# Gate product in four parts, square in two, and a rescheduled first layer, in a two-layer image kernel

## The chip, the cores and the metric

The kernel runs on one core of a Trainium2 chip. The metric is the device time of one execution in microseconds (us), the median of several runs. The engines are named as in the profile: PE (TensorE, matrix products; its weight loads are listed apart as PEld), DVE (VectorE), ACT (ScalarE), POOL (GpSimd) and SP (SyncE, which issues nearly all transfers). Each engine works through its own queue in order.

## The reference

The input is a batch of 4 images with 128 channels and 64 x 64 pixels. Layer 0 is a convolutional block with state-space branches, layer 1 is attention with a mixture of experts. All of it is in float32. The change lies in layer 0, whose core is the gated scan that the reference calls `_mamba`:

```python
def _mamba(x, in_w, in_b, conv_w, conv_b, A_log, D, dt_bias, rms_w, out_w, headdim, d_state):
    zxbcdt = x @ in_w.T + in_b
    z = zxbcdt[..., :di]
    xBC = zxbcdt[..., di:2 * di + 2 * d_state]
    dt = jax.nn.softplus(zxbcdt[..., -nh:] + dt_bias)
    xBC = sum((xp[:, k:k + l, :] * conv_w[:, k] for k in range(K)))
    xBC = _silu(xBC + conv_b)
    ...
    y = _ssd(xs * dt[..., None], dt * A, Bm, Cm)
    y = y + D[None, None, :, None] * xs
    y = y.reshape(b, l, di) * _silu(z)
    y = y * jax.lax.rsqrt(jnp.mean(y * y, -1, keepdims=True) + 1e-05) * rms_w
    return y @ out_w.T

def _ssd(x, A, Bm, Cm, chunk=64):
    Lmat = jnp.exp(_segsum(A))
    Yd = jnp.einsum('bcln,bcsn,bhcls,bcshp->bclhp', Cm, Bm, Lmat, x)
    dec = jnp.exp(Acs[..., -1:] - Acs)
    states = jnp.einsum('bcln,bhcl,bclhp->bchpn', Bm, dec, x)
    ...
    Yo = jnp.einsum('bcln,bchpn,bhcl->bclhp', Cm, prev, jnp.exp(Acs))
    return (Yd + Yo).reshape(b, l, h, p)
```

The line `y.reshape(b, l, di) * _silu(z)` is the gate product of the title, and `y * y` in the line below it is the square. Around the branches, layer 0 has a group norm, a projection to 8 seed channels, layer norms and, per image, a convolution block: a product that widens 128 channels to 256, a 3 x 3 depthwise convolution, a gelu and a product back to 128.

## The kernel before

**Tiling.** A sequence of 4096 pixels is worked on in 8 blocks of 512 positions (`LB`), and a block in chunks of 64 (`Q`). One item is one block of one scan. There are 72 items: 8 of the seed scan (all four images together, 4 lanes) and 64 of the cascade (two scans in a row for each of 4 images and 8 blocks, 8 lanes). For a cascade item the main tiles hold 128 partitions x 1024 elements, for a seed item 128 x 512: four parts `u` (`NU` = 4) of 256 or 128 elements.

**Stages of an item** (class `Mamba`). `outer` loads and normalizes the block. `prep` loads it again with its halo (tile `x4`, four transfers on SP's queue from the scratch tensor `hl`) and makes the decays: `ps_dt`, `u`, `sd`, the scan `acs`, and `cdx`, `ps_cd`, `cds`. `front` computes z, x, B and C on PE (`ps_z`, `ps_x`, `ps_B`, `ps_C`), each closed by a silu on ACT; then the transposes `pt_b` and `pt_x`, the products `ps_g` with their mask (tile `gm`), the states `ps_st`, the two scans `cd` over them on DVE (with the small product `inj` and an addition into `ps_st` between the first and the second), and `ps_yo`, the part of y that comes from earlier states. The state at the end of an item is kept in `last` for the next item of the same scan. `back` does the part inside the chunks and the closing.

**The closing of `back`.** For each part `u`, `exponentials(u)` makes the decay factors e (PE `ps_d`, then an exponential on ACT), `weigh(u)` multiplies them by `gm` on DVE, and `within(u)` multiplies them with x on PE and adds the result to y on DVE, in four instructions. In the profile the psum tiles of `within` are named `bank` and in the code `py`. After all four parts, one POOL instruction multiplies the gate into the whole tile (`zs` <- `y`, `zs`), one ACT instruction squares it (`y` <- `zs`), PE takes the mean (`ps_ms`, four instructions), ACT makes the reciprocal root out of it, and PE the product `ps_out`.

**The order of the work** in layer 0 is neither written out by hand nor left to the compiler. The class `Deck` records every instruction with the tiles that it reads and writes; `flush` then plays a model of the five engines and emits the instructions in the order in which the model starts them. Each operation has a price (`price`; `SIDE` holds PE's prices for some psum tiles). When an operation ends, those that need it become ready after `LAG` us on another engine; what a transfer brings is ready `LAND` us after it. Among the ready operations of an engine the one of the highest rank goes first. The rank is the place in the record, moved back by `BEHIND`, a table by stage, engine and tile: 120 means "as if recorded 120 places later", -200 means earlier. `NEAR` lets PE look, among operations of nearly the same rank, for one of the same shape of weights; it is 0. `lockers` keeps POOL's instructions and DVE's with two inputs in SBUF from running at the same time in the model. The rest follows from the rings of buffers: a tile can be opened only when one of its ring is free.

**Layer 0's end and layer 1.** The convolution block (function `ffn`) of one image runs beside the scans of the next. For the last image there is no next: its block runs alone with the first projections of layer 1 (`early`), recorded and flushed separately. In it `merge(k)` loads and normalizes block k into a tile of the ring `outs`, `expand` and the taps compute on it, and `close` finishes the block and frees the tile. `depth` adds buffers to the rings `outs` and `acc`; `load` fetches input blocks into the ring `xg`. Layer 1 is written in a fixed order and isn't touched.

Of the kernel before, what the change touches and what calls it, by code (L numbers as in the profile page):

```python
# [20 lines left out]
F32 = mybir.dt.float32  # L21
# [10 lines left out]
LB = 512  # L32
# [243 lines left out]
class Mamba:  # L276
# [344 lines left out]
    def back(self, it, out):  # L621
# [59 lines left out]
        for u in range(NU):  # L681
            within(u)
            if u + 1 < NU:
                weigh(u + 1)
            if u + 2 < NU:
                exponentials(u + 2)
            yield


        nc.gpsimd.tensor_mul(zs, y, zs)  # L690
        yield
        yield
        nc.scalar.activation(y, zs, AF.Square)
        yield
# [69 lines left out]

SIDE = {"py": 0.0435, "ps_yo": 0.033, "ps_d": 0.08}


class Deck:
# [67 lines left out]
    def price(self, engine, name, args, kw, out, ins, op):  # L836
# [26 lines left out]
        if engine == "gpsimd":  # L863
            return 0.15 + 0.0023 * n
        quick = name in ("tensor_scalar", "tensor_copy") and len(sb) == 1 and out.space == bass.MemoryType.SB
# [6 lines left out]
    BEHIND = {  # L872
        ("back", "gpsimd", "last0_casc1"): 120, ("back", "scalar"): -50, ("back", "scalar", "A_casc1"): -200,
        ("back", "scalar", "e"): -40, ("back", "sync", "gfd"): -10, ("back", "sync", "hl"): 120,
        ("back", "sync", "raw"): -40, ("back", "sync", "td"): 110, ("back", "tensor", "ps_d"): -70,
        ("back", "tensor", "py"): 120, ("back", "vector", "A_casc1"): -200, ("back", "vector", "bdt_casc1"): 70,
        ("back", "vector", "biasB_casc1"): 40, ("back", "vector", "wc_casc1"): -120, ("ffn", "scalar"): 10,
        ("ffn", "tensor", "ps_mean"): 40, ("ffn", "vector", "acc"): 140, ("front", "gpsimd"): 220,
        ("front", "gpsimd", "last_casc1"): -10, ("front", "scalar"): 20, ("front", "scalar", "Bc"): 50,
        ("front", "scalar", "Cc"): -200, ("front", "scalar", "cd"): 200, ("front", "scalar", "zs"): -70,  # L880
        ("front", "tensor"): 20, ("front", "tensor", "ps_ea"): -120, ("front", "tensor", "ps_g"): -120,
        ("front", "tensor", "ps_st"): -20, ("front", "tensor", "pt_x"): 40, ("front", "vector", "gm"): 10,
        ("front", "vector", "ps_st"): -20, ("front", "vector", "xd"): -200, ("front", "vector", "xp0"): -10,
        ("outer", "gpsimd"): -200, ("outer", "gpsimd", "halo_seed"): 200, ("outer", "gpsimd", "last0_casc0"): 120,
        ("outer", "scalar"): 40, ("outer", "scalar", "hi"): -120, ("outer", "scalar", "ln_r"): -20,
        ("outer", "sync", "raw"): 20, ("outer", "sync", "wc_seed"): 20, ("outer", "sync", "xin"): -40,
        ("outer", "tensor"): 110, ("outer", "tensor", "ps_tok"): 40, ("outer", "vector"): -20,
        ("outer", "vector", "A_seed"): 200, ("outer", "vector", "W_casc0"): 200, ("outer", "vector", "bdt_casc0"): 10,
        ("outer", "vector", "bdt_seed"): 10, ("outer", "vector", "biasB_casc0"): 20,
        ("outer", "vector", "biasB_seed"): -10, ("outer", "vector", "biasx_seed"): 200,  # L890
        ("outer", "vector", "raw"): 70, ("prep", "gpsimd"): 70, ("prep", "gpsimd", "cdx"): 10,
        ("prep", "gpsimd", "halo_seed"): 10, ("prep", "gpsimd", "x4"): -40, ("prep", "scalar", "cde"): -70,
        ("prep", "sync", "x4"): 40, ("prep", "tensor", "ps_cd"): 10, ("prep", "vector", "acs"): -190,
        ("prep", "vector", "sdT"): -70,
    }
    LAG = 0.2
    NEAR = 0
    LAND = 4.0

    def flush(self, tc):  # L900
# [29 lines left out]
        for i, op in enumerate(ops):  # L930
            if op.waits == 0:
                heappush(events, (0.0, 0, i))
        now, table, lock, mode = 0.0, None, None, None
        lockers = {"vector": 0.0, "gpsimd": 0.0}
        while events:
# [16 lines left out]
            for e in engines:  # L952
# [3 lines left out]
                while ready[e]:  # L956
# [12 lines left out]
                    if any(room[r] < k for r, k in need.items()) or any(  # L969
# [6 lines left out]
                        continue  # L976
                    if e == "tensor" and chosen is None and op.mode != mode:

                        chosen = key
                        continue  # L980
                    if chosen is not None and (op.mode != mode or key[0] - chosen[0] > self.NEAR):
                        aside.append(key)
                        if key[0] - chosen[0] > self.NEAR:
                            break
                        continue
                    if chosen is not None:
                        aside.append(chosen)
                    chosen = key
# [16 lines left out]
                if e == "tensor" and op.mode != mode:  # L1005
                    mode = op.mode
                    start += 0.1
                if e == "scalar":
                    if op.set == SILU:
                        phases[op.phase] -= 1  # L1010
                        lock = op.phase if phases[op.phase] else None
                    if op.set is not None and op.set != table:
                        table = op.set
                        start += 1.3
                end = start + op.cost
                busy[e] = end
# [128 lines left out]
def layer0(tc, T, td, const, ident, eps, where, batches, qkv):  # L1145
# [9 lines left out]
    with ExitStack() as ctx:  # L1155
# [62 lines left out]

        def load(b, k, work=work):
            xin = work.tile([128, LB], F32, tag="xg", bufs=4, name="xin")  # L1220
            nc.sync.dma_start(out=xin, in_=T["x"][b, :, blk(k)])
            return xin
# [125 lines left out]
        def ffn(b, work, ps, depth=0, diag=0, taps=None, ps_taps=None):  # L1348
# [18 lines left out]
            def merge(k):  # L1367
# [13 lines left out]
                nc.sync.dma_start(out=gf, in_=gfd[32 * b:32 * b + 8, blk(k)])  # L1381
                xg = load(b, k, work)
                yield
# [49 lines left out]
            def conv(k):  # L1433

                accs[k] = []
                for g in range(2):
                    acc = work.tile([128, LB], F32, tag="acc", bufs=3 + depth, name="acc")
                    sums = made[k].pop(0) if k in made else None
                    for i in range(diag, 9):
                        w = P("dw")[:, 9 * g + i:9 * g + i + 1]  # L1440
                        if sums is None:
                            nc.vector.tensor_scalar(rows(acc), tap(g, i), w, None, ALU.mult)
                        else:
                            nc.vector.scalar_tensor_tensor(rows(acc), tap(g, i), w, sums, ALU.mult, ALU.add)
                        sums = rows(acc)
                        if i % 3 == 2:
                            yield
                    accs[k].append(acc)

            def close(k):  # L1450
# [4 lines left out]
                nc.scalar.preload_act_table_set(LNEXP)  # L1455
                xin = load(b, k, work)
                yield
# [73 lines left out]

        pending = deck.staged("ffn", ffn(pending, last, single("f", 4), 0, 4, taps, single("t", 2)))
        run((pending, FFN), (deck.staged("early", early()), 5 * NBLK + 7))
# [503 lines left out]
```

## Time and profile before

Three runs took 8400.1, 8414.19 and 8424.57 us: a median of 8414.19 us.

| | before |
|---|---|
| median of three runs | 8414.19 us |
| the profiled execution | 8410.01 us |
| its span, first to last instruction | 8408.0 us |
| granted TensorE clock over the span | 0.948 |
| busy over the span: PE / DVE / ACT / POOL | 7635.6 / 6326.8 / 5095.5 / 4737.9 us |
| gate product `zs` on POOL, 64 cascade items | 160.8 us, 2513 ns each |
| square `y` <- `zs` on ACT, 63 of the cascade items | 66.6 us, 1057 ns each |
| `ps_ms` on PE, 252 instructions of cascade items | 118.7 us busy |
| `ps_out` on PE, as many, the same shapes | 79.6 us busy |

The first five rows are of the whole execution; the others are of the stretch from 150 to 3550 us, which holds nearly all of the items. The profile records one execution. Its times are microseconds, "mean ns" is the mean of one instruction. Every recorded instruction of layer 0 carries line 1031, since the scheduler emits them all there; so groups are told apart by the names of their tiles. "Idle before, and what ended it" gives the time that an engine stood still ahead of the instructions of a group, and the instruction on another engine that released it. The granted clock is the share of its full rate at which PE was allowed to run.

### The profile page before, as it was taken

How to read it: one execution, taken by the hardware profiler on the slowest of the kernel's cores; microseconds unless marked ns; L12 is line 12 of the kernel's file. 1: busy time of each engine (PE TensorE's matmuls, PEld its weight loads, DVE VectorE, ACT ScalarE, POOL GpSimd, SP SyncE). 2: the span in 40 equal slices, each digit the busy share in tenths (PEclk: the TensorE clock that was granted, in tenths of full speed). 3: DMA queues.
4: the chain of work that ended last, by engine and by line, in shares of the span. 5: the costliest groups of instructions: out<-in, count | busy, mean ns of one | idle time of the engine just before them, and what ended most of it. 6: DMA issues, size and time to landing. Idle time of an engine off the chain costs nothing.

```text
span 8408.0 us, 191225 instructions
## 1 busy us (share of the span) xinstructions
PE 7635.6 (91%) x80284; PEld 4548.2 (54%) x80284; DVE 6326.8 (75%) x11211; ACT 5095.5 (61%) x6444; POOL 4737.9 (56%) x3225
## 2 busy tenths in 40 slices
PE   5888888888888888789999999999999999999998
PEld 3566666666666666534554555555555545555554
DVE  6767667887788788767777777777777777777775
ACT  5767677777777777654555555555555555555554
POOL 1111111111111111107999999999999999999997
PEclk8899899988999999889999999999999999999999
DMA  4211111121121112135454545454545545444442
GB/s 143 84 51 45 54 47 50 54 56 50 51 58 52 51 54 57 34 122 132 125 133 125 130 118 138 120 127 128 127 122 132 131 120 131 118 119 119 120 120 60
DMA packets 306604, 800.54 MB, mean 95 GB/s; under 512 B 43984, under 2 KB 61008, under 8 KB 288848
## 3 DMA queue, kind: packets, MB, share of 16 engines
q1 hardware_dynamic: 304848, 780.94, 35.3%
q8 instruction: 633, 10.37, 0.5%
q10 hardware_dynamic: 432, 5.12, 0.2%
q0 software_dynamic: 464, 2.25, 0.1%
q14 instruction: 227, 1.86, 0.1%
HBM read 595.19 MB, written 192.94 MB: 94 GB/s over the span
## 4 chain that ended last, share of the span: by engine, by line
PE 51%; POOL 25%; DVE 10%; ACT 7%; issue 5%; DMA 2%; SPq 0%; POOLq 0%; DVEq 0%; ACTq 0%
POOL s L1885 14%; PE ps_mx L1841 7%; POOL es L1887 6%; PE acc L1900 6%; PE ps_s L1879 5%; PE bank L1031 4%; PE ps_s L1873 3%; PE ps_x L1031 2%; PE ps_B L1031 2%; PE ps_d L1031 2%; DVE y L1031 2%; PE ps_C L1031 2%; PE ps_yo L1031 2%; DVE e L1031 2%; POOL zs L1031 1%
## 5 line engine op out<-in xcount | busy, mean ns | idle before, releaser
L1843 DVE TENSOR_REDUCE mx<-ps_mx 128x1 f32<-128x512 f32 x4096 | 2789.4, 688 | 818.8 <-PE ps_mx L1841 811.4
L1883 ACT ACTIVATE e<-ps_s 128x1024 f32<-128x1024 f32 x2048 | 1985.9, 1022 | 1723.9 <-PE ps_s L1879 1604.5
L1885 POOL TENSOR_TENSOR s<-e 128x1024 f32<-128x1024 f32 x1024 | 2442.8, 2386 | 210.4 <-ACT e L1883 205.0
L1841 PE MATMUL ps_mx<-k,q 128*128 128x512 f32 x4096 | 1879.3, 468 | 57.4 <-DVE mx L1843 23.2
L1887 POOL TENSOR_TENSOR es<-s 128x512 f32<-128x512 f32 x1024 | 1312.1, 1281 | 80.3
L1879 PE MATMUL ps_s<-q,k 128*128 128x512 f32 x4096 | 1281.7, 394 | 0.0
L1900 PE MATMUL acc<-e,V 128*32 128x512 f32 x8192 | 1096.3, 607 | 0.0
L1841 PEld LDWEIGHTS ps_mx<-k,q 128*128 128x128 f32 x4096 | 774.9, 189 | 528.7 <-DVE mx L1843 216.9
L1879 PEld LDWEIGHTS ps_s<-q,k 128*128 128x128 f32 x4096 | 773.3, 189 | 138.6 <-issue 2.7
L1031 DVE SCALAR_TENSOR_TENSOR e<-e,gm 128x1024 f32<-128x1024 f32 (+1 forms) x576 | 663.3, 1162 | 28.8 <-ACT e L1031 27.3
L1873 PEld LDWEIGHTS ps_s<-mr,ones 32*128 32x128 f32 x4096 | 200.4, 181 | 889.9 <-ACT e L1883 414.7
L1031 ACT ACTIVATE e<-ps_d 128x1024 f32<-128x1024 f32 (+1 forms) x576 | 547.0, 974 | 111.3 <-PE ps_d L1031 92.1
L1031 POOL TENSOR_TENSOR u<-acs 128x512 f32<-128x512 f32 x72 | 74.8, 1039 | 926.5 <-DVE acs L1031 907.2
L1031 DVE SCALAR_TENSOR_TENSOR y<-bank,const,y 128x128 f32<-128x128 f32 (+1 forms) x1152 | 365.8, 336 | 266.1 <-PE bank L1031 264.2
L1873 PE MATMUL ps_s<-mr,ones 32*128 32x512 f32 x4096 | 531.5, 496 | 20.3 <-ACT e L1883 20.3
L1031 PE MATMUL bank<-e,xp 64*32 64x128 f32 x17408 | 473.3, 283 | 62.6 <-DVE y L1031 59.1
L1031 PE MATMUL ps_d<-rt,lt 32*128 32x256 f32 x4352 | 422.4, 317 | 52.1 <-ACT y L1031 15.1
L1031 PEld LDWEIGHTS bank<-e,xp 64*32 64x32 f32 x17408 | 373.1, 110 | 145.7 <-DVE y L1031 99.3
L1031 PEld LDWEIGHTS ps_d<-rt,lt 32*128 32x128 f32 x4352 | 306.4, 195 | 222.3 <-ACT e L1031 49.9
L1900 PEld LDWEIGHTS acc<-e,V 128*32 128x32 f32 x8192 | 161.4, 108 | 363.5 <-issue 356.0
L1031 PE MATMUL ps_ms<-y,const 128*64 128x512 f32 (+1 forms) x272 | 133.7, 1033 | 237.7 <-ACT y L1031 233.7
L1031 POOL TENSOR_TENSOR zs<-y,zs 128x1024 f32<-128x1024 f32 (+1 forms) x72 | 173.6, 2411 | 311.1 <-DVE y L1031 311.0
(349 smaller groups left out, 11961.3 us busy)
## 6 DMA issues: line engine op xcount, KB each, us to landing
k<-kd SPq DMA_DIRECT2D x512, 512.0 KB, 7.1
x<-hl SPq DMA_DIRECT2D x256, 256.0 KB, 5.1
V<-vd SPq DMA_DIRECT2D x128, 512.0 KB, 11.4
cd<-raw SPq DMA_DIRECT2D x256, 256.0 KB, 5.2
parts<-cd SPq DMA_DIRECT2D x128, 512.0 KB, 5.6
xin<-in_x SPq DMA_DIRECT2D x128, 256.0 KB, 3.6
q<-qd SPq DMA_DIRECT2D x512, 64.0 KB, 4.5
hl<-hi SPq DMA_DIRECT2D x72, 256.0 KB, 2.0
```

The costliest lines, as they stand in the source:

```text
L1031: getattr(getattr(self.nc, op.engine), name)(*[self.real(a) for a in args], **{k: self.real(a) for k, a in kw.items()})
L1841: nc.tensor.matmul(p, lhsT=q4s[u][:, 128 * qt:128 * qt + 128], rhs=k4s[u][:, blk(kb)], start=True, stop=True)
L1843: nc.vector.tensor_reduce(mxs[u][:, qt, kb:kb + 1], p, AX.X, ALU.max)
L1873: nc.tensor.matmul(pts[j // 2][:, j % 2, :], lhsT=ones2[rows, :], rhs=mrows[u][rows, :], start=True, stop=False)
L1879: nc.tensor.matmul(pts[j // 2][:, j % 2, :], lhsT=k4s[u][:, 128 * kt:128 * kt + 128], rhs=q4s[u], start=False, stop=True)
L1883: nc.scalar.activation(e[:, 2 * j:2 * j + 2], pts[j], AF.Exp)
L1885: nc.gpsimd.tensor_add(s2, e[:, 0:2], e[:, 2:4])
L1887: nc.gpsimd.tensor_add(s, s2[:, 0], s2[:, 1])
L1900: nc.tensor.matmul(accs[u][32 * j:32 * j + 32, :], lhsT=Vs[u][:, 4 * g + j, :], rhs=e[:, j, :], start=g == 0, stop=g == 7)
```

## The change

One POOL instruction for the gate becomes four, each issued by the loop over `u` once the part is complete; the square becomes two instructions of half the size. The number of stages that `back` yields stays 13. In the scheduler, the prices of `ps_d` and of POOL's instructions are other ones, `LAG` is 0.05 in place of 0.2, the loop that looks for PE operations of the same shape is taken out, and PE's operations cost twice as much where PE has been idle for more than 2 of the last 4 us (`COLD`). `BEHIND` holds more and other moves. In the separate block at the end, `ffn` gets a `depth` of 1 in place of 0, so `outs` has four buffers there in place of three; `acc` keeps three, and `xg` gets three there in place of four.

```diff
@@ -684,13 +685,17 @@
                 weigh(u + 1)
             if u + 2 < NU:
                 exponentials(u + 2)
+
+            part = slice(256 * ng // 2 * u, 256 * ng // 2 * (u + 1))
+            nc.gpsimd.tensor_mul(zs[:, part], y[:, part], zs[:, part])
             yield
-        nc.gpsimd.tensor_mul(zs, y, zs)
-        yield
-        yield
-        nc.scalar.activation(y, zs, AF.Square)
+        yield
+        yield
+        half = 256 * ng
+        for part in (slice(0, half), slice(half, 2 * half)):
+            nc.scalar.activation(y[:, part], zs[:, part], AF.Square)
         yield
         def by_token(t):
@@ -762,7 +767,7 @@
 SILU, GELU, EXPS = "silu", "gelu", "exps"
-SIDE = {"py": 0.0435, "ps_yo": 0.033, "ps_d": 0.08}
+SIDE = {"py": 0.0435, "ps_yo": 0.033, "ps_d": 0.072}
 class Deck:
@@ -861,7 +866,7 @@
                 return 0.375 + 0.00085 * n
             return (0.28 if is_ap(kw.get("bias")) else 0.2) + 0.0008 * n
         if engine == "gpsimd":
-            return 0.15 + 0.0023 * n
+            return 0.15 + (0.00174 if name == "tensor_sub" else 0.00225) * n
         quick = name in ("tensor_scalar", "tensor_copy") and len(sb) == 1 and out.space == bass.MemoryType.SB
         op.both = len(sb) > 1 or quick
         if name == "tensor_tensor_scan":
@@ -870,31 +875,37 @@
     BEHIND = {
-        ("back", "gpsimd", "last0_casc1"): 120, ("back", "scalar"): -50, ("back", "scalar", "A_casc1"): -200,
-        ("back", "scalar", "e"): -40, ("back", "sync", "gfd"): -10, ("back", "sync", "hl"): 120,
-        ("back", "sync", "raw"): -40, ("back", "sync", "td"): 110, ("back", "tensor", "ps_d"): -70,
-        ("back", "tensor", "py"): 120, ("back", "vector", "A_casc1"): -200, ("back", "vector", "bdt_casc1"): 70,
-        ("back", "vector", "biasB_casc1"): 40, ("back", "vector", "wc_casc1"): -120, ("ffn", "scalar"): 10,
-        ("ffn", "tensor", "ps_mean"): 40, ("ffn", "vector", "acc"): 140, ("front", "gpsimd"): 220,
-        ("front", "gpsimd", "last_casc1"): -10, ("front", "scalar"): 20, ("front", "scalar", "Bc"): 50,
-        ("front", "scalar", "Cc"): -200, ("front", "scalar", "cd"): 200, ("front", "scalar", "zs"): -70,
-        ("front", "tensor"): 20, ("front", "tensor", "ps_ea"): -120, ("front", "tensor", "ps_g"): -120,
-        ("front", "tensor", "ps_st"): -20, ("front", "tensor", "pt_x"): 40, ("front", "vector", "gm"): 10,
-        ("front", "vector", "ps_st"): -20, ("front", "vector", "xd"): -200, ("front", "vector", "xp0"): -10,
+        ("back", "gpsimd"): 70, ("back", "gpsimd", "last0_casc1"): 120, ("back", "scalar"): -50,
+        ("back", "scalar", "A_casc1"): -200, ("back", "scalar", "e"): -40, ("back", "sync"): 40,
+        ("back", "sync", "gfd"): -10, ("back", "sync", "hl"): 120, ("back", "sync", "raw"): -40,
+        ("back", "sync", "td"): 110, ("back", "tensor", "ps_d"): -70, ("back", "tensor", "ps_out"): 120,
+        ("back", "tensor", "py"): 120, ("back", "vector", "A_casc1"): -200, ("back", "vector", "bdt_casc1"): 140,
+        ("back", "vector", "biasB_casc1"): 40, ("back", "vector", "biasC_casc1"): 200, ("back", "vector", "raw"): 10,
+        ("back", "vector", "wc_casc1"): -120, ("ffn", "gpsimd", "h1_1"): 70, ("ffn", "scalar"): 10,
+        ("ffn", "sync", "gf8"): 30, ("ffn", "tensor", "ps_gmix"): 10, ("ffn", "tensor", "ps_mean"): 40,
+        ("ffn", "tensor", "ps_var"): 10, ("ffn", "vector", "acc"): 140, ("ffn", "vector", "t"): -40,
+        ("front", "gpsimd", "last_casc1"): -10, ("front", "scalar"): 20, ("front", "scalar", "Bc"): -20,
+        ("front", "scalar", "Cc"): -400, ("front", "scalar", "bT"): -40, ("front", "scalar", "cd"): 240,
+        ("front", "scalar", "rt"): -10, ("front", "scalar", "zs"): -70, ("front", "tensor"): 20,
+        ("front", "tensor", "ps_ea"): -120, ("front", "tensor", "ps_g"): -120, ("front", "tensor", "ps_st"): 180,
+        ("front", "tensor", "ps_x"): 20, ("front", "tensor", "ps_z"): -10, ("front", "tensor", "pt_x"): 40,
+        ("front", "vector", "gm"): 20, ("front", "vector", "ps_st"): -20, ("front", "vector", "xd"): -200,
+        ("front", "vector", "xp0"): -10, ("front", "vector", "xp3"): 30, ("front", "vector", "y"): -200,
         ("outer", "gpsimd"): -200, ("outer", "gpsimd", "halo_seed"): 200, ("outer", "gpsimd", "last0_casc0"): 120,
         ("outer", "scalar"): 40, ("outer", "scalar", "hi"): -120, ("outer", "scalar", "ln_r"): -20,
-        ("outer", "sync", "raw"): 20, ("outer", "sync", "wc_seed"): 20, ("outer", "sync", "xin"): -40,
-        ("outer", "tensor"): 110, ("outer", "tensor", "ps_tok"): 40, ("outer", "vector"): -20,
-        ("outer", "vector", "A_seed"): 200, ("outer", "vector", "W_casc0"): 200, ("outer", "vector", "bdt_casc0"): 10,
-        ("outer", "vector", "bdt_seed"): 10, ("outer", "vector", "biasB_casc0"): 20,
-        ("outer", "vector", "biasB_seed"): -10, ("outer", "vector", "biasx_seed"): 200,
-        ("outer", "vector", "raw"): 70, ("prep", "gpsimd"): 70, ("prep", "gpsimd", "cdx"): 10,
-        ("prep", "gpsimd", "halo_seed"): 10, ("prep", "gpsimd", "x4"): -40, ("prep", "scalar", "cde"): -70,
-        ("prep", "sync", "x4"): 40, ("prep", "tensor", "ps_cd"): 10, ("prep", "vector", "acs"): -190,
+        ("outer", "scalar", "xin"): 200, ("outer", "sync", "raw"): 20, ("outer", "sync", "wc_seed"): -10,
+        ("outer", "sync", "xin"): -40, ("outer", "tensor"): 110, ("outer", "tensor", "ps_tok"): 40,
+        ("outer", "vector"): -20, ("outer", "vector", "A_seed"): 200, ("outer", "vector", "W_casc0"): 200,
+        ("outer", "vector", "bdt_casc0"): 10, ("outer", "vector", "bdt_seed"): 10,
+        ("outer", "vector", "biasB_casc0"): 20, ("outer", "vector", "biasB_seed"): -10,
+        ("outer", "vector", "biasx_seed"): 200, ("outer", "vector", "raw"): 70, ("outer", "vector", "wc_casc0"): 10,
+        ("prep", "gpsimd"): 190, ("prep", "gpsimd", "cdx"): 10, ("prep", "gpsimd", "halo_seed"): 10,
+        ("prep", "gpsimd", "x4"): -40, ("prep", "scalar", "ah"): -40, ("prep", "scalar", "cde"): -70,
+        ("prep", "sync", "x4"): 90, ("prep", "tensor", "ps_cd"): 10, ("prep", "vector", "acs"): -190,
         ("prep", "vector", "sdT"): -70,
     }
-    LAG = 0.2
-    NEAR = 0
+    LAG = 0.05
+    COLD = 4.0, 2.0
     LAND = 4.0
     def flush(self, tc):
@@ -930,7 +941,7 @@
         for i, op in enumerate(ops):
             if op.waits == 0:
                 heappush(events, (0.0, 0, i))
-        now, table, lock, mode = 0.0, None, None, None
+        now, table, lock, mode, worked = 0.0, None, None, None, deque()
         lockers = {"vector": 0.0, "gpsimd": 0.0}
         while events:
             now = events[0][0]
@@ -974,17 +985,6 @@
                             e == "gpsimd" and lockers["vector"] > now + 1e-9):
                         aside.append(key)
                         continue
-                    if e == "tensor" and chosen is None and op.mode != mode:
-
-                        chosen = key
-                        continue
-                    if chosen is not None and (op.mode != mode or key[0] - chosen[0] > self.NEAR):
-                        aside.append(key)
-                        if key[0] - chosen[0] > self.NEAR:
-                            break
-                        continue
-                    if chosen is not None:
-                        aside.append(chosen)
                     chosen = key
                     break
                 for key in aside:
@@ -1005,6 +1005,13 @@
                 if e == "tensor" and op.mode != mode:
                     mode = op.mode
                     start += 0.1
+                if e == "tensor":
+
+                    span, most = self.COLD
+                    while worked and worked[0][1] < start - span:
+                        worked.popleft()
+                    busy_for = sum(b - max(a, start - span) for a, b in worked)
+                    slow = 2 if span - busy_for > most else 1
                 if e == "scalar":
                     if op.set == SILU:
                         phases[op.phase] -= 1
@@ -1012,7 +1019,9 @@
                     if op.set is not None and op.set != table:
                         table = op.set
                         start += 1.3
-                end = start + op.cost
+                end = start + op.cost * (slow if e == "tensor" else 1)
+                if e == "tensor":
+                    worked.append((now, end))
                 busy[e] = end
                 if op.both or e == "gpsimd":
                     lockers[e] = end
@@ -1216,8 +1225,8 @@
         sh.psy = Halves(deck, scan.enter_context(tc.tile_pool(name="psy", bufs=1, space=PSUM)))
         gfd = dram.tile([128, L], F32, name="gfd")
-        def load(b, k, work=work):
-            xin = work.tile([128, LB], F32, tag="xg", bufs=4, name="xin")
+        def load(b, k, work=work, bufs=4):
+            xin = work.tile([128, LB], F32, tag="xg", bufs=bufs, name="xin")
             nc.sync.dma_start(out=xin, in_=T["x"][b, :, blk(k)])
             return xin
@@ -1379,7 +1388,7 @@
                 nc.scalar.activation(r, y, AF.Square)
                 gf = work.tile([128, LB], F32, tag="ys", name="gf8")[0:8, :]
                 nc.sync.dma_start(out=gf, in_=gfd[32 * b:32 * b + 8, blk(k)])
-                xg = load(b, k, work)
+                xg = load(b, k, work, 4 - depth)
                 yield
                 pv = ps("ps_var")
                 nc.tensor.matmul(pv, lhsT=const("avg"), rhs=r, start=True, stop=True)
@@ -1434,7 +1443,7 @@
                 accs[k] = []
                 for g in range(2):
-                    acc = work.tile([128, LB], F32, tag="acc", bufs=3 + depth, name="acc")
+                    acc = work.tile([128, LB], F32, tag="acc", bufs=3, name="acc")
                     sums = made[k].pop(0) if k in made else None
                     for i in range(diag, 9):
                         w = P("dw")[:, 9 * g + i:9 * g + i + 1]
@@ -1453,7 +1462,7 @@
                 for g, a in enumerate(acc):
                     nc.scalar.activation(a, a, AF.Gelu_apprx_tanh, bias=P("dw_b")[:, g:g + 1])
                 nc.scalar.preload_act_table_set(LNEXP)
-                xin = load(b, k, work)
+                xin = load(b, k, work, 4 - depth)
                 yield
                 pf = ps("ps_f")
                 for g in range(2):
@@ -1529,7 +1538,7 @@
         def single(tag, bufs):
             return lambda name: pp.tile([128, LB], F32, tag=tag, bufs=bufs, name=name)
-        pending = deck.staged("ffn", ffn(pending, last, single("f", 4), 0, 4, taps, single("t", 2)))
+        pending = deck.staged("ffn", ffn(pending, last, single("f", 4), 1, 4, taps, single("t", 2)))
         run((pending, FFN), (deck.staged("early", early()), 5 * NBLK + 7))
         deck.flush(tc)
```

More of the change, by code (lines that the diff above doesn't have):

```diff
@@ L10 @@
 from contextlib import ExitStack
+from collections import deque
 from heapq import heappop, heappush
```

## The prediction, made before the changed kernel ran

> **What bounds the kernel now.** I read first the busy time by stretches (columns: from:to, length, busy time and instructions of each engine, granted clock, DMA share, GB/s), cut at the borders of the stages: seeds, the cascade items, the last convolution block, attention.
>
> ```profile
> 0.00:422.00 422.00, 297.10 (x4508) 195.06 (x4508) 278.49 (x642) 274.25 (x435) 56.98 (x98) 0.85 0.35 113
> 422.00:3552.00 3130.00, 2663.00 (x49806) 1931.72 (x49804) 2401.10 (x3943) 2244.65 (x2920) 403.22 (x468) 0.91 0.18 51
> 3552.00:3790.00 238.00, 178.08 (x443) 77.06 (x443) 151.38 (x229) 122.44 (x194) 17.30 (x19) 0.85 0.39 123
> 3790.00:8408.00 4618.00, 4497.46 (x25535) 2344.33 (x25533) 3495.81 (x6400) 2454.18 (x2896) 4260.40 (x2640) 0.99 0.48 122
> ```
>
> The change touches nothing behind 3790 us: those 4618 us stay. In the 3130 us of cascade items PE is busy 2663 us (85%) at a clock of 0.91, DVE 77%, ACT 72%, POOL 13%. PE idles 467 us there. What it waits for is in the list of PE's waits in that stretch:
>
> ```profile
> PE ps_ms L1031 <- ACT y L1031: 222.5, 54, 7.6
> PE bank L1031 <- DVE y L1031: 54.6, 83, 2.4
> PE ps_st L1031 <- issue: 33.7, 40, 2.0
> PE ps_yo L1031 <- DVE cd L1031: 33.0, 18, 4.0
> ```
>
> Nearly half of the idle time is one wait, before `ps_ms`. One item in order of time shows its chain:
>
> ```profile
> 562.88 0.34 DVE L1031 SCALAR_TENSOR_TENSOR y<-bank,const,y 128x128 f32<-128x128 f32 x1
> ...
> 563.30 2.35 POOL L1031 TENSOR_TENSOR zs<-y,zs 128x1024 f32<-128x1024 f32 x1 [0.34 <-DVE y L1031]
> 563.47 1.21 DVE L1031 TENSOR_TENSOR_SCAN cd<-cd,ps_st 128x512 f32<-128x512 f32 x1
> 564.60 1.20 DVE L1031 TENSOR_TENSOR gm<-ps_g,const 128x1024 f32<-128x1024 f32 x1
> ...
> 565.68 1.06 ACT L1031 ACTIVATE y<-zs 128x1024 f32<-128x1024 f32 x1 [1.97 <-POOL zs L1031]
> 565.71 0.56 DVE L1031 TENSOR_TENSOR inj<-cd,cds 128x128 f32<-128x128 f32 x1
> ...
> 566.79 1.98 PE L1031 MATMUL ps_ms<-y,const 128*64 128x512 f32 x4 [4.28 <-ACT y L1031]
> 567.12 1.22 DVE L1031 TENSOR_TENSOR_SCAN cd<-cd,ps_st 128x512 f32<-128x512 f32 x1
> ...
> 568.70 0.90 PE L1031 MATMUL ps_cd<-cdx,const 128*128 128x160 f32 x2
> ...
> 569.53 0.65 PE L1031 MATMUL ps_yo<-Cc,last_casc 64*32 64x64 f32 x16
> ```
>
> The last y ends at 563.22; gate product 2.35, square 1.06, then `ps_ms`. PE stood 4.28 us. A second chain runs beside: the scans of `cd` end at 568.34, and `ps_yo` needs them; it starts at 569.53. So `ps_yo` can gain 1.2 us here, however early `ps_ms` comes. Handoffs are short: zs ends at 565.65 and the square starts at 565.68, which ends at 566.74, and PE starts at 566.79.
>
> **The change, part by part.**
>
> Gate and square, cascades. The forms of two sizes give the quarters and halves:
>
> ```profile
> L1031 POOL TENSOR_TENSOR zs<-y,zs x72: 1279/2350/3202, 126.5 to 3548.0; 128x1024 f32<-128x1024 f32 x64, 128x512 f32<-128x512 f32 x8
> L1031 ACT ACTIVATE y<-zs x72: 617/1057/1058, 128.2 to 3550.8; 128x1024 f32<-128x1024 f32 x64, 128x512 f32<-128x512 f32 x8
> ```
>
> The minima are those of 512 elements, the medians those of 1024. A line through 1.279 and 2.350 gives 0.21 us plus 2.09 ns an element: a quarter of 256 takes 0.74. Half a square is 0.62. Behind the last y stand 0.74 + 0.62 = 1.36 us in place of 3.41: 2.05 saved. If every one of the 54 waits gave that, 54 x 2.05 = 111 us. The lower bound goes item by item through the timeline: the least of 2.05, the item's own wait, and the gap from the end of `cd` to the start of `ps_yo` (median 1.4 us); that sums to about 81 us. I take 90, near the lower end, since only `inj` in the second chain gets quicker.
>
> Seeds: their gate goes from 1.28 to 0.48 (128 elements by the same line), the square from 0.62 to 0.40 (a line through 617 and 1057): 1.02 saved in each of six waits of 2.0 to 2.4 us (two of them put down to DVE): 6 us.
>
> Half clock. `ps_ms` took 1.97 or 1.98 us behind 49 of the 54 waits, and 1.08 behind those of 0.58, 1.94 and 2.55 us: the slow clock followed waits from 2.32 us on. With 2.05 off each, 19 stay above that; 30 x 0.90 = 27 us (0 if `ps_yo` waits for `cd` anyway).
>
> What the smaller pieces add. POOL: 4 x 0.74 - 2.35 = 0.6 us an item, on an engine 13% busy; ACT 2 x 0.617 - 1.057 = 0.18 us, with the first half inside the loop: nothing, as long as ACT has its 28% free; else 62 x 0.18 = 11 us. Dearer is the place. The pieces now run between the `weigh` steps. The trace has instructions held by a neighbour: `inj` on DVE takes 0.38 us in the median and up to 1.46, `sd<-sd,u`, two tiles of SBUF multiplied, 0.67 to 2.84, and the gate itself 2.35 in most items but 3.19 in nine; those that read PSUM beside the gate (scan, `gm`) stay at 1.21. `weigh` (e and gm, 1.22 us) reads two SBUF tiles. Three pieces an item meet it; if each holds DVE for its 0.74, 63 x 3 x 0.74 = 140 us; if DVE's 23% idle time takes them, 0. I take 45, a third, because DVE is off the path in most of the item and `bank` waits only 54.6 us for it. In POOL's queue halo copies, `u`, `cdx`, `inj` and `last` now stand behind pieces that wait for y; ACT's wait for `u` is 16 us today, `cdx` feeds only `ps_cd`.
>
> A rule speaks against this part: the Trainium skill, GPSIMD Engine Reference, section Key points, says that POOL shares its SBUF interfaces with VectorE and collides with instructions of two SBUF inputs. The rows above agree for `inj` and `sd`; taken strictly, for every meeting, the sum below would hold +140 in place of +45 and come out at 8383.
>
> The scheduler. New prices, a lag of 0.05 for 0.2, a half clock and new moves do no work themselves; they change each engine's queue. The handoffs above (0.03 to 0.05 us) suit 0.05, and 0.15 + 0.00225 x 1024 = 2.45 us for the gate is near 2.35. The loop taken out of TensorE's choice held only for equal ranks (NEAR is 0), so its going costs nothing. Moves: `Cc`'s silu and the y of `ps_yo` go ahead, `ps_st` goes back by 200 places, which can delay `cd` and with it `ps_yo`; SP's loads of x4 go back by 50, four per item with 5.1 us to landing. What waits for those is POOL's halo copy (461 us idle, off the path) and then `ps_dt`; if that slack is gone, up to 5.1 us an item. Bounds: a gain of the other idle time of PE, 467 - 222 = 245 us; a loss of one `cd` wait (33.0 / 18 = 1.83 us) in each of 62 items, 114 us. I take a gain of 40, a sixth of the way: holes such as `gm` standing between the two scans (1.2 us) can be closed, but every hole has its own chain.
>
> The last block (238 us): a fourth buffer for `outs`, one fewer for `xg`. PE waits there 6.0 us for loads of `outs` and 10.0 for `ln_r`: at most 16 gained, at worst 10 lost to loads of xin; 8 gained.
>
> Sum: -90 - 6 - 27 - 40 - 8 + 45 = -126. The profiled execution took 8410 us (span 8408); the median of the runs is 8414, 4 above it. 8410 - 126 + 4 = 8288.
>
> **The rivals.** First, the second chain takes over: `ps_yo` waits for `cd`, `ps_st` moved back makes that later, and of the sum stay the gate at half its lower bound and the seeds: 8414 - 41 - 6 = 8367. For it: `cd` ends behind the start of `ps_ms` in nearly all items. Against: the gap to `ps_yo` still has 1.4 us.
>
> Second, slower: the pieces and `weigh` hold each other. Place: the loop over u, between y and the next `bank`. A piece waits for the 1.22 us of a `weigh`, then the next `weigh` waits for the piece: 189 x 1.22 = 231 us. Gains left: 90 + 6 + 8 = 104, so 8414 + 231 - 104 = 8541. From a hold of 0.55 us a piece (104 / 189) on, the gain is eaten; from 0.68 (129 / 189) the kernel is measurably slower. For it: `sd` at 2.84. Against: POOL is free 87% and y itself reads PSUM.
>
> Third, the order closes much more: 110 of the 245 us, gate 111, clock 27, seeds 6, last block 16, no holds: 8414 - 270 = 8144.
>
> Fourth, the change doesn't do what it says: queues differ so that the hole before `ps_ms` stands elsewhere, 8414.
>
> **How the numbers follow.** The forecast has 0.48, the second chain 0.20, the wide gain 0.07, nothing 0.09, slower 0.16. What the measurement can tell from no change is 0.3%, 25 us: under 8389 is faster (0.48 + 0.20 + 0.07 = 0.75), to 8439 the same (0.09), above slower (0.16). The range runs from the wide gain, 8145, to 8440; the forecast's own from 8173 (order 110, holds 0) to 8383 (holds 140).
>
> **What would show it.** Right: the wait of `ps_ms` for ACT under 130 us, `ps_ms` nearer 1.1 us for four, the clock at 0.92 or above, PE under 2640 us in the same items, which end some 110 us sooner. The second chain: `ps_yo` waiting for `cd` 80 us and more. The slower case: `weigh` longer than 1.22 on average, `bank` waiting for DVE over 150 us. Wrong altogether: a new wait of PE that is in none of these rows, or a change behind the last block.

## The result, and the profile after

The changed kernel took 8309 us (median of four runs), the kernel before 8412 us beside it: 0.9875 of the time, 95% interval 0.9863 to 0.9887, or 103 us less. The forecast was 8288 us.

The busy time by stretches, changed kernel, from the first cascade item's `ps_ms` to the last one's, then the last convolution block:

```profile
424.00:3467.00 3043.00, 2643.00 (x49938) 1903.08 (x49940) 2378.62 (x3960) 2251.85 (x2984) 540.69 (x660) 0.93 0.19 52
3467.00:3691.00 224.00, 175.03 (x440) 77.03 (x436) 146.22 (x219) 124.00 (x195) 16.56 (x19) 0.84 0.40 128
```

The cascade items took 3130 us and take 3043: 87 of the 103 us. PE's idle time there went from 467 to 400 us, and its busy time, for the same instructions, from 2663 to 2643, at a clock of 0.93 in place of 0.91. The last block, from the last `ps_ms` to the first product of the attention, went from 236.0 to 226.4 us. What PE waits for in the cascade stretch, with the same columns as before:

```profile
PE ps_ms L1040 <- ACT y L1040: 131.0, 53, 8.8
PE bank L1040 <- DVE y L1040: 49.8, 54, 1.4
PE ps_g L1040 <- DVE gm L1040: 21.1, 18, 1.7
PE ps_st L1040 <- DVE gm L1040: 20.8, 17, 2.5
...
PE ps_cd L1040 <- POOL cdx L1040: 15.8, 6, 2.9
PE ps_yo L1040 <- DVE cd L1040: 7.9, 6, 2.7
```

The wait of `ps_ms` for the square fell by 91 us (222.5 to 131.0). `ps_ms` now also waits for other work, 17 us in all, so that the idle time before it fell by 75 (222.5 to 147.9). The wait of `ps_yo` for the scans fell by 25. Waits for `gm` (ahead of `ps_g` and `ps_st`) and for `cdx` came up by some 45: before, `cdx` stood in no row, and those for `gm` were

```profile
PE ps_g L1031 <- DVE gm L1031: 6.8, 14, 0.7
PE ps_st L1031 <- DVE gm L1031: 6.4, 5, 2.1
```

One item in order of time:

```profile
573.50 0.33 DVE L1040 SCALAR_TENSOR_TENSOR y<-bank,const,y 128x128 f32<-128x128 f32 x1
...
573.75 1.04 POOL L1040 TENSOR_TENSOR u<-acs 128x512 f32<-128x512 f32 x1 [3.62 <-DVE acs L1040]
...
574.75 0.72 POOL L1040 TENSOR_TENSOR zs<-y,zs 128x256 f32<-128x256 f32 x1
...
575.51 0.63 ACT L1040 ACTIVATE y<-zs 128x512 f32<-128x512 f32 x1
576.19 1.97 PE L1040 MATMUL ps_ms<-y,const 128*64 128x512 f32 x4 [3.08 <-ACT y L1040]
...
578.05 1.22 DVE L1040 TENSOR_TENSOR_SCAN cd<-cd,ps_st 128x512 f32<-128x512 f32 x1
...
578.95 1.97 PE L1040 MATMUL ps_out<-zs,wc_casc 128*64 128x512 f32 x4
...
580.85 0.65 PE L1040 MATMUL ps_yo<-Cc,last_casc 64*32 64x64 f32 x16
```

The last quarter (0.72 us) and half a square (0.63) are as long as forecast, but the quarter finds POOL taken by `u` for 0.9 us: from the last y to `ps_ms` it is now 2.4 us, not 3.6 and not 1.4. And `ps_yo` starts 7.0 us behind the last y where it started 6.3 us behind it: `ps_out` now goes ahead of it. So this item, from the early part in which no convolution block runs beside the scans, won nothing, and the part as a whole little. Stretches of equally many items show it, first of before:

```profile
422.00:1332.00 910.00, 769.64 (x14904) 573.06 (x14900) 628.53 (x1048) 637.27 (x822) 103.94 (x133) 0.91 0.17 47
...
1332.00:3522.00 2190.00, 1873.35 (x34568) 1346.42 (x34568) 1748.11 (x2858) 1592.93 (x2080) 295.15 (x332) 0.91 0.19 53
```

And of the changed kernel:

```profile
425.00:1329.00 904.00, 771.87 (x15038) 563.92 (x15040) 620.99 (x1050) 639.64 (x836) 136.29 (x189) 0.91 0.17 47
...
1329.00:3431.00 2102.00, 1846.41 (x34432) 1322.36 (x34428) 1724.95 (x2861) 1595.20 (x2127) 393.99 (x462) 0.93 0.20 55
```

The first 19 items went from 910 to 904 us, the 43 behind them from 2190 to 2102: there PE's idle time fell from 317 to 256 us and its busy time from 1873 to 1846. A likely reason is that a convolution block gives PE other work to put into a hole that got shorter; no run shows that apart.

### The profile page after: what moved, and what is told of

Its sections match the earlier page's. It is cut to its first block, busy times and chain, and to the rows that moved or that the text cites. A ratio compares the mean times of both kernels' runs of the same rounds, so it can differ in the third digit from the quotient of the medians.

```text
span 8309.0 us, 191474 instructions
## 1 busy us (share of the span) xinstructions
PE 7600.4 (91%) x80284; PEld 4516.6 (54%) x80284; DVE 6299.9 (76%) x11211; ACT 5103.8 (61%) x6517; POOL 4892.5 (59%) x3441
## 4 chain that ended last, share of the span: by engine, by line
PE 29%; POOL 22%; issue 3%; DVE 2%; ACT 1%; DMA 1%; SPq 0%; POOLq 0%; DVEq 0%
POOL s L1894 13%; PE ps_mx L1850 7%; PE acc L1909 6%; POOL es L1896 6%; PE ps_s L1888 6%; PE ps_s L1882 3%; PE ps_e L1798 2%; PE ps_den L1922 1%; DVE mx L1852 1%; PE ps_taps L1040 1%; PE ps_sh L1869 0%; POOL parts L1712 0%; POOL cx L1714 0%; PE ps_f L1787 0%; PE ps_f L1786 0%
## 5 line engine op out<-in xcount | busy, mean ns | idle before, releaser
L1040 POOL TENSOR_TENSOR zs<-y,zs 128x256 f32<-128x256 f32 (+1 forms) x288 | 302.7, 1052 | 1153.0 <-DVE y L1040 1152.2
L1805 DVE SCALAR_TENSOR_TENSOR acc<-ps_e,w,acc 128x128 f32<-128x128 f32 x896 | 312.5, 349 | 47.7 <-PE ps_e L1798 15.0
L1040 DVE SCALAR_TENSOR_TENSOR acc<-h,pb,acc 128x512 f32<-128x512 f32 x448 | 330.4, 757 | 7.5
```

Source lines behind the costliest of these rows:

```text
L1040: getattr(getattr(self.nc, op.engine), name)(*[self.real(a) for a in args], **{k: self.real(a) for k, a in kw.items()})
L1805: nc.vector.scalar_tensor_tensor(acc, pe[:, 128 * j:128 * j + 128], we, acc, ALU.mult, ALU.add)
```

## The experiments

The change has three parts that can be set apart: the split of gate and square, the model (prices, lag, half clock, and the last block's buffers with it), and the moves. The first seven runs take them apart, the others look into the model and into the moves. Every time is a median; the kernel before ran beside each at 8406 to 8412 us.

**The split alone.**

```diff
+            nc.gpsimd.tensor_mul(zs[:, part], y[:, part], zs[:, part])
...
-        nc.gpsimd.tensor_mul(zs, y, zs)
...
-        nc.scalar.activation(y, zs, AF.Square)
...
+        for part in (slice(0, half), slice(half, 2 * half)):
+            nc.scalar.activation(y[:, part], zs[:, part], AF.Square)
```

> The kernel before with the gate in four parts and the square in two, its scheduler and moves untouched. Theory A (the shorter chain behind the last y pays by itself): 60 to 110 us faster than before, so 8300 to 8350 us, with the wait of ps_ms for ACT down from 222 us to some 120 to 140. Theory B (the second chain, the scans of cd, takes over as long as the queues stay): at most 47 us faster, 8365 us or more, and ps_yo waits for cd 80 us and more. Theory C (the parts and weigh hold each other): not faster than before, the mean of weigh over 1.30 us.

8397 us, ratio 0.9986 (0.9977 to 0.9996): some 9 to 12 us won. The wait that the split aims at did halve. PE's waits in its cascade items (this profiled execution took 8428 us, 31 above the median, so its lines tell the kind of wait better than the sum):

```profile
PE ps_ms L1035 <- ACT y L1035: 109.7, 45, 5.3
PE ps_yo L1035 <- DVE cd L1035: 73.1, 41, 3.0
PE bank L1035 <- DVE y L1035: 37.4, 47, 2.1
PE ps_g L1035 <- DVE gm L1035: 29.3, 23, 2.4
```

`ps_yo` now waits 73 us for the scans, 33 before. One item shows how:

```profile
617.23 1.21 DVE L1035 TENSOR_TENSOR_SCAN cd<-cd,ps_st 128x512 f32<-128x512 f32 x1
...
618.50 0.72 PE L1035 MATMUL ps_yo<-Cc,cd 64*32 64x64 f32 x32 [1.51 <-DVE cd L1035]
...
619.56 0.63 ACT L1035 ACTIVATE y<-zs 128x512 f32<-128x512 f32 x1 [2.39 <-POOL zs L1035]
...
621.59 2.36 PE L1035 MATMUL ps_yo<-Cc,cd 64*32 64x64 f32 x80 [2.37 <-DVE cd L1035]
...
625.04 1.98 PE L1035 MATMUL ps_ms<-y,const 128*64 128x512 f32 x4
```

The square is done at 620.2, but `ps_ms` stands behind `ps_yo` (and a `ps_d` that follows it) in PE's queue, and `ps_yo` waits for both scans: `ps_ms` starts at 625.0. PE has `ps_yo` ahead of `ps_ms` in 18 of the 64 cascade items here, in 10 before and in none of the changed kernel. By its time this is Theory B, with a wait of 73 us where it asked for 80; Theory A falls, and so does C: `weigh` takes 1231 ns in the mean.

But the second chain is only a part of where the gain went. The wait of `ps_yo` grew by 40 us, while that of `ps_ms` fell by 113. In the cascade items PE idles 419 us, 48 less than before, and is busy for 2729 us, 66 more, for the same instructions, at a granted clock of 0.90 in place of 0.91. The same two stretches as above, the first 19 items and the 43 behind them:

```profile
430.00:1382.00 952.00, 814.98 (x15044) 595.47 (x15042) 628.06 (x1055) 641.30 (x843) 162.27 (x191) 0.86 0.16 45
1382.00:3542.00 2160.00, 1890.74 (x34296) 1353.27 (x34294) 1726.68 (x2843) 1595.97 (x2121) 390.21 (x459) 0.91 0.19 53
```

The first 19 items are 42 us longer than before, with as much idle time (137 us for 140) and 45 us more of busy time, at a clock of 0.86 for 0.91. So much of what the split saves in waiting is lost again in slower matrix products. By how much in a median execution isn't known, and neither is why PE met the half clock more often.

**The scheduler without the split.** The changed kernel with gate and square whole:

```diff
-            nc.gpsimd.tensor_mul(zs[:, part], y[:, part], zs[:, part])
...
+        nc.gpsimd.tensor_mul(zs, y, zs)
...
```

> The changed kernel with the gate and the square whole again: new prices, lag, half clock, moves and buffers alone. Theory A: 10 to 45 us faster than before (8365 to 8400 us), with the wait of ps_ms for ACT still near 200 us. Theory B (the queues bring the gain): 55 to 100 us faster, 8312 to 8357 us. A third case: slower than before, since the moves were found for the split gate.

8493 us, ratio 1.0102 (1.0085 to 1.0119): slower by about 87 us, the third case. Its largest waits:

```profile
PE ps_ms L1036 <- ACT y L1036: 131.9, 53, 5.1
PE ps_st L1036 <- DVE gm L1036: 87.9, 28, 4.9
PE bank L1036 <- DVE y L1036: 72.8, 86, 4.4
PE ps_dt L1036 <- DMA x<-hl: 28.0, 8, 4.4
```

`ps_st` waits 88 us for `gm` (6 before, 21 in the changed kernel), and `ps_dt` 28 us for its loads, of which the kernel before had 1.4 us in all. The new moves send `ps_st` and those loads back, which fits; no run undid them singly. PE's busy time in the cascade items is up too, from 2663 to 2733 us, at a clock of 0.89.

**The last block's buffers.**

```diff
...
-        pending = deck.staged("ffn", ffn(pending, last, single("f", 4), 1, 4, taps, single("t", 2)))
+        pending = deck.staged("ffn", ffn(pending, last, single("f", 4), 0, 4, taps, single("t", 2)))
...
```

> The changed kernel with the buffers of the last convolution block as before (outs three, xg four). If the fourth buffer of outs made the last block 14 us shorter (238 to 224 us), this is 8 to 16 us slower than the changed kernel, 8317 to 8325 us; if the new scheduler did it, within 4 us of it, 8305 to 8313 us.

8315 us, 0.9892 (0.9876 to 0.9909); from the last `ps_ms` to the first product of the attention 235.8 us, as before the change (236.0), where the changed kernel takes 226.4. The medians differ by 6 us, and by 12 when each is set against the kernel before of its own round; the intervals overlap. The stretch says that the fourth buffer is worth 9 us.

**The moves of before in the changed kernel.** The table `BEHIND` of before; all else stays new.

> The changed kernel with the table of moves of before; the gate, the prices, the lag, the half clock and the buffers stay new. If the moves carry little, 8310 to 8335 us; if they carry the scheduler's share, 8340 to 8400 us; if the moves of before are wrong for the new record and lag, above 8412 us.

8364 us, 0.9949 (0.9932 to 0.9965), so the moves carry the scheduler's share: 54 us of the 103 by the medians, 61 against the kernel before of each round.

**The model alone, the moves alone, split and moves without the model.** The kernel before with the other parts put in:

```diff
...
-    LAG = 0.2
-    NEAR = 0
+    LAG = 0.05
+    COLD = 4.0, 2.0
...
```

> Gate and square whole, moves of before, but the new prices, lag, half clock and the last block's buffers. Additive theory (each part has its own worth, whatever stands beside it): gate and model together were 42 us faster, the gate alone 9, so the model alone is worth 33 us: 8365 to 8385 us. Interaction theory (the gain comes from queues that fit the short chain, and the model alone orders work round a chain that is still long): not faster than before, 8395 to 8450 us.

8367 us, 0.9947 (0.9932 to 0.9963): 45 us won, in the range of the additive theory.

> The kernel before with the new table of moves alone. Additive theory: the moves were worth 54 us in the changed kernel, so 8345 to 8370 us. Interaction theory: the moves are fitted to the split gate and the short lag, so here they are worth nothing or cost, 8410 to 8500 us; as the scheduler alone cost 87 us, I expect 8450.

8430 us, 1.0020 (1.0010 to 1.0031): 17 us lost, the interaction theory.

> The kernel before with the split gate and square and the new moves, but the old lag, prices and no half clock. Additive theory: 9 + 54 us faster, 8340 to 8355 us. Interaction theory: the moves need the model that they were found with, 8370 to 8430 us.

8416 us, 1.0005 (0.9994 to 1.0015): nothing won, the interaction theory again. Its PE waits 80 us at `ps_yo` for `cd`, with `ps_yo` first in 19 of 64 items.

All eight combinations together, in brackets the difference to the kernel before that ran beside each:

| | moves of before | new moves |
|---|---|---|
| whole gate, old model | 8412 | 8430 (+18) |
| split gate, old model | 8397 (-9) | 8416 (+3) |
| whole gate, new model | 8367 (-45) | 8493 (+87) |
| split gate, new model | 8364 (-42) | 8309 (-103) |

By these differences the model, with the moves of before, is worth 34 to 45 us, and the split 9 with the old model and nothing with the new one. The new moves cost 12 to 132 us in three rows and win 61 in the one that they go with.

**The lag.** The changed kernel with `LAG = 0.2`.

> The changed kernel with the lag back at 0.2. If the lag matters because the handoffs in the trace take 0.03 to 0.05 us, 20 to 60 us slower than the changed kernel, 8330 to 8370 us. If it is only one of many settings that shuffle the order, within 15 us of it either way, 8294 to 8324 us.

8365 us, 0.9946 (0.9928 to 0.9964): 56 us slower than the changed kernel. `ps_yo` stands ahead of `ps_ms` in 14 of 64 items, and it waits again:

```profile
PE ps_ms L1040 <- ACT y L1040: 101.0, 42, 5.0
PE ps_yo L1040 <- DVE cd L1040: 52.6, 33, 2.7
```

By the code, the chain from y to `ps_ms` crosses engines three times (POOL, ACT, PE) and pays the lag each time, while the scans stay on DVE and pay it once, at the end. At 0.2 the model therefore sees `cd` ready first more often, and the counts agree (14 items and none). The waits, though, mostly moved from one place to another: PE idles 405 us in the cascade items, 400 in the changed kernel, and is busy 2683 us for 2643, at a clock of 0.91 for 0.93. The moves were there with the lag of 0.05, so a part of the 56 us may be theirs; with the moves of before the two states of the lag weren't run apart from the rest of the model.

**The half clock.** The changed kernel with `slow = 1` in every case.

> The changed kernel with the half clock out of the scheduler (PE's operations never cost double). If the half clock in the model matters as much as the lag did (56 us), 8350 to 8380 us; if it only shuffles the order away from what the moves were found for, 8315 to 8350 us; if it is idle, within 6 us of 8309.

8310 us, 0.9883 (0.9864 to 0.9903): idle, as far as the time goes.

**Moves found for each gate.** The same random search, some 600 trials each from the table of before under the new model, once with the whole and once with the split gate. It kept 15 changes for the whole and 20 for the split one, among these last:

```diff
...
+        ('front', 'tensor', 'ps_x'): 360,
...
+        ('back', 'tensor', 'ps_ms'): -120,
+        ('ffn', 'tensor', 'ps_var'): -160,
...
+        ('front', 'vector', 'y'): -120,
...
```

> Gate and square whole, the new prices, lag, half clock and buffers, and moves found for this record by some 600 random trials from the table of before (a move is kept when it shortens the scheduler's own model). Theory D (the gate is worth something once the moves are found for it): this stays behind the same search with the split gate by 15 to 45 us, 8330 to 8360 us. Theory E (the gate in parts is worth nothing, any record with moves of its own gets there): within 12 us of the split one, 8300 to 8335 us. Theory F (moves from the model do not carry to the chip): 8355 to 8400 us, no faster than the model alone (8367).

8361 us, 0.9941 (0.9924 to 0.9959): 6 us better than the model with the moves of before, so Theory F for this one.

> The same search, as many trials, with the gate in four parts and the square in two. Theory D: 8300 to 8335 us, 15 to 45 us ahead of the one with the whole gate. Theory E: within 12 us of it. Theory F: 8350 us or more, no faster than gate and model with the moves of before (8363).

8267 us, 0.9830 (0.9811 to 0.9849): 94 us ahead of the whole gate, and 42 ahead of the changed kernel. Theory D, with more than twice the size expected. PE's largest waits from 430 us to the last `ps_ms`, of the whole gate and then of the split one, each with its own moves:

```profile
PE ps_ms L1078 <- ACT y L1078: 178.7, 57, 5.2
PE bank L1078 <- DVE y L1078: 60.5, 71, 3.3
PE ps_yo L1078 <- DVE cd L1078: 32.5, 20, 4.0
```

```profile
PE ps_ms L1088 <- ACT y L1088: 129.7, 54, 9.8
PE bank L1088 <- DVE y L1088: 45.8, 45, 2.5
PE ps_g L1088 <- DVE gm L1088: 27.1, 23, 1.7
...
PE ps_ms L1088 <- DVE cd L1088: 23.5, 6, 3.9
...
PE ps_yo L1088 <- DVE cd L1088: 11.6, 7, 2.1
```

The three waits that both lists have are 85 us apart, while others grew (`ps_ms` for `cd`, `ps_g` for `gm`). Over the cascade items PE idles 454 us with the whole gate and 391 with the split one, and is busy 2677 and 2641 us. Not all of the 94 us is the gate's: the search moved operations of the last convolution block as well, which has no gate, and from the last `ps_ms` to the first product of the attention these two kernels take 227.9 and 208.5 us. So 19 of the 99 us between the two profiled executions lie there, and some 80 ahead of it. One search of each kind was made, so how far chance enters isn't known.

**More trials from the changed kernel's table.**

> The changed kernel with as many trials more from its own table. If the model's gains carry to the chip, 10 to 25 us faster than the changed kernel, 8284 to 8299 us; if they are spent, within 8 us of it; if a move fits the model alone, slower than 8317 us.

8275 us, 0.9836 (0.9816 to 0.9856): 34 us faster than the changed kernel, more than expected. Both searched kernels beat the changed one; the split gate with moves of its own (8267 us) is the fastest of this study.

## Why the forecast held, point by point

The sum was -126 us and the result -103: sign and size were right. But two of its terms were not separate things, and their errors met; that the sum came so near is in part luck.

- **Gate and square, -90 and -6.** The durations were right (quarter 0.72 for 0.74, half square 0.63 for 0.62), and so was the wait: 222 us down to 131, where under 130 was forecast. As a saving in time it was wrong by itself: alone it gave about 10 us. The step that failed is the bound "item by item through the timeline": it took the gap between `cd` and `ps_yo` as it stood in the old queues, with `ps_ms` ahead of `ps_yo`. The scheduler sorts anew when the chain gets shorter: it put `ps_yo` first in 18 items, where it had been first in 10, and the wait of `ps_yo` grew by 40 us. That is the first rival, the second chain; with the old lag it comes back each time (73, 80 and 53 us of waiting in three runs). The other part was in no rival: in the profiled execution of the split alone PE's busy time in the items rose by 66 us, where the half-clock term had it fall by 27. With moves found for each gate the split is worth up to 94 us, near the forecast for a reason that the forecast didn't give. Of the 6 us for the seeds nothing is seen: the first cascade item's `ps_ms` starts at 424.9 us, where it started at 422.2.
- **The order, -40.** Mis-sized: the new model, with the last block's buffers in it, gave 45 alone, and the moves another 54 to 61 in the changed kernel. It isn't a term beside the gate's: the moves pay only with this split and this model, and cost up to 132 us without.
- **Half clock, -27.** Wrong for the chain that it was worked out for: it moved. Four `ps_ms` took 1.6 us or more in 56 of the 64 items before and in 36 now, four `ps_out` in 14 before and in 36 now. So `ps_ms` became faster (119.8 to 100.9 us busy in the cascade items), and `ps_out` by as much slower (79.6 to 101.7), as in the item above, where it runs at 1.97 us in the same slow stretch. Before and after:

```profile
L1031 PE MATMUL ps_ms<-y,const 128*64 128x512 f32 x254 | 119.8, 1041 | 222.5 <-ACT y L1031 222.5
L1031 PE MATMUL ps_out<-zs,wc_casc 128*64 128x512 f32 x252 | 79.6, 715 | 0.4
...
L1040 PE MATMUL ps_out<-zs,wc_casc 128*64 128x512 f32 x252 | 101.7, 896 | 7.8 <-DVE t L1040 2.6 <-ACT y L1040 1.7 <-ACT ln_r L1040 1.4
L1040 PE MATMUL ps_ms<-y,const 128*64 128x512 f32 x254 | 100.9, 884 | 147.9 <-ACT y L1040 131.0 <-DVE cd L1040 7.9 <-DVE inj L1040 6.1
```

  PE's busy time in the items did fall by 20 us, but in other products (`ps_d` 376.9 to 364.5 us, `bank` 436.3 to 426.0, `ps_x` 198.8 to 188.5).
- **The port, +45.** Mis-sized: `weigh` went from 1222 to 1236 ns, 504 x 14 ns = 7 us. The pieces collide with it, but mostly POOL pays. First `weigh` before, then `weigh` and the pieces after:

```profile
L1031 DVE SCALAR_TENSOR_TENSOR e<-e,gm 128x1024 f32<-128x1024 f32 x504 | 611.2, 1222 | 24.2 <-ACT e L1031 23.1
...
L1040 DVE SCALAR_TENSOR_TENSOR e<-e,gm 128x1024 f32<-128x1024 f32 x504 | 615.2, 1236 | 50.1 <-ACT e L1040 49.0
L1040 POOL TENSOR_TENSOR zs<-y,zs 128x256 f32<-128x256 f32 x253 | 270.8, 1071 | 1011.2 <-DVE y L1040 1010.5
```

  A piece takes 1071 ns in the mean where its undisturbed length is 720 to 740. The step that failed is "three pieces an item meet it": by the trace 57 of the 256 pieces overlap a `weigh`. The scheduler's model keeps the two apart (`lockers`), which fits. In 42 meetings the `weigh` had begun first, and the piece took 1.76 us in the mean; in 18 the piece had, and the `weigh` took 1.40 us in place of 1.22. The rule of the Trainium skill (GPSIMD Engine Reference, Key points), that POOL contends for SBUF with VectorE's instructions of two SBUF inputs, is seen here too, in the pieces' length. Taken as a cost to DVE at every meeting (140 us) it would have been wrong by 133 us. The slower rival fell with it.
- **The last block, -8.** Right: 9 us.
- **The signs named.** The items end 85 us sooner for 110 forecast, clock 0.93 for 0.92 or more, PE busy 2643 for under 2640, `ps_ms` for ACT 131 for under 130, and four `ps_ms` still at the half clock in 36 of 64 items, where nearer 1.1 us was forecast.

## What to carry to other kernels

Where an order is worked out by a program, shortening one chain is not a saving that can be read off the old timeline: ask which work the scheduler will put first once the chain is shorter, and what then waits in the same queue. Tuned priorities belong to the record and the model with which they were found; measure an edit with the priorities found anew, or it is judged by the misfit (the split: 10 us with the old ones; with its own up to 94, some 80 of them outside the last block). Look at PE's busy time beside its waits: the same products can take longer (2729 us for 2663), and a wait that was saved is then paid there. A shared port has a payer: look how often the two engines' instructions meet, and which of them get longer, before the collision is booked on the path.

## What was not expected of the hardware

Handoffs between engines are short in these traces: from the end of one instruction to the start of the next 0.03 us from POOL to ACT, 0.05 from ACT to PE and 0.08 from DVE to POOL. To let the scheduler count 0.2 us in their place cost 56 us of 8309, with the moves held.

In the kernel before, the half clock mostly followed PE's waits from about 2.3 us on (49 of 54 waits, as the prediction read them). In the changed kernel the length of the wait just before `ps_ms` doesn't tell it: the four products took 1.6 us or more behind eleven waits of 0.92 to 2.20 us, and at most 1.15 us, the full clock, behind four waits of 2.41 to 3.39. What decides it stays open here. Whether the scheduler knows of the half clock made no difference (8310 for 8309 us).
